# Two-layer vision kernel: the routing of the next batch is emitted between z and the FFN of the current one

## The chip, the cores and the metric

The kernel runs on one core of a Trainium2 chip. Its engines are TensorE (PE, matmuls; PEld is its weight load), VectorE (DVE), ScalarE (ACT), GpSimd (POOL) and SyncE (SP, which issues most DMAs). The metric is the device time of one launch in microseconds. The kernel before takes 4330.48 us, the median of three runs (4320.04 to 4338.9).

## What is computed

Four images of 384 channels and 32x32 pixels go through two layers in float32. Each layer is a mixing step and a feed-forward step, both with a residual.

```python
# layer 0
x = x + gelu(layernorm(selective_scan_in_four_directions(ln_c(x))))
t = to_tokens(x)                                   # 4 x 1024 tokens of 384
probs = softmax(ln_t(t) @ gate_w + gate_b)         # 4 experts, the best 2 of them kept
masked = probs * top2 ; masked /= masked.sum() + 1e-9
t = t + sum_e masked[e] * (gelu(ln_t(t) @ w1[e] + b1[e]) @ w2[e] + b2[e])
# layer 1
w = ln_c(x) @ w_qkv.T                              # one matrix serves as q, k and v; 8 heads of 64
x = x + softmax(w w.T / 8) w @ w_out.T + b_out
h = gelu(ln_t(t) @ kron(c_fc_1, c_fc_2).T)         # 384 -> 1536, a Kronecker product of rank 1 on one side
t = t + h @ kron(c_proj_1, c_proj_2).T
```

The scan is a recurrence over 1024 positions with 16 states for each of 384 channels, in four directions.

## The kernel before

The work has two parts for each batch (image).

The **scan** (`scan_layer`) walks 4 batches x 4 directions x 2 halves of the positions. A unit of these has three blocks of 128 channels (`chunk`), and a chunk four groups of states. For each group POOL multiplies step size and B (`bx`, L440, and L468 for C on half of them), ACT takes the exponential `da` (L449), DVE runs the recurrence (L454) and multiplies by C (L461), and PE adds up the states into `acc` (L475). One such group is called a scan step below; a batch has 96. The inputs of a chunk come through DRAM in SP's queue (`dtr` L424, `bcs` L350, `dd` L405 and L406), with seven `dtr` buffers. `acc` lives in PSUM, `bx` has six buffers.

The **tail** of a batch is everything after its scan:
- `route`: zero the table of rows (`clear`, L610), load x1 (L649), transpose it on PE together with the gate's scores (`tt_ps`, L656), evict (ACT L642, DVE L643), take token statistics on DVE (L662), store the tokens (L664). Then rank the experts of each token (`places`: a chain of some 70 small DVE operations, with two matmuls `cnt_ps` at L753), load the tokens again (L677), normalise them on ACT (L678) and scatter each token to its two rows by indirect DMAs from POOL (L683, 16 of them).
- `experts`: eleven slots of 256 or 128 rows, each of one expert, known only at run time (L866 loads its number into SP). Weights (L875, L883), a gather (L899), its transposes (`xc_ps`, L910), two matmul blocks (L927, L942) with a gelu between.
- `combine` and `prologue`: gather the two results of a token and weigh them, then normalise and transpose.
- `attention`: scores L1051, exponential on ACT L1057, weighted sum L1097, and at the end of each pair of heads the division (L1073).
- `last_layers`: for each half, output projection plus residual (`o_ps`, L1149 and L1151), a normalisation across channels that ends in `z` (L1158 to L1180), and after both halves the FFN: `h_ps` (L1193), gelu (L1202), `f_acc` (L1210), `fo_ps` (L1218), output (L1221).

Engines take their instructions in order, so the order in the program decides. It isn't written out by hand: a scheduler places each instruction on its engine's queue by data dependences, by a priority (the order of emission, with `high_priority(offset=FORWARD)` moving a block ahead by 20000) and by a timeline that it keeps for itself. `between(b)` calls `tail_batch(b - 1)` after the scan of batch b, and the scheduler then lays the tail over the scan of the next batch. The tail of batch 3 comes last, with nothing beside it but what the tail of batch 2 has left.

The order of emission in a tail is: experts, combine, prologue, attention, then `between()`, which for batches 0 and 1 emits the routing of the next batch, and then `last_layers`. So the routing of batch 1 is emitted ahead of the last layers of batch 0, both with the same offset of priority.

Buffers: tag `k4` has five tiles of 3 KB per partition (`NARROW`). `x` and `xt` of the routing, `xs`, `xc` and `y` of the experts, `ex` of the attention, `xt`, `z`, `fy` and `out` of the last layers all take theirs from it. PSUM tiles of the tail come from tag p (three banks) and tag o (one bank), `NARROW_BANKS`. The ranking's scratch area `places` takes the bank of tag o for its whole length, and so do `y_ps`, `o_acc` and `f_acc`. Tag `kw` (eight tiles of 4.5 KB) holds expert weights, and in turn attention's `w`, `vt` and `att` and the last layers' `wa`, `wb` and `wc`.

Of the kernel before, what the change touches and what calls it, by code (L numbers as in the profile page):

```python
# [18 lines left out]
B = 4  # L19
# [66 lines left out]
FORWARD = 20000  # L86
# [25 lines left out]
def halves(i):  # L112
    return slice(i * HF, (i + 1) * HF)


class Body:
# [380 lines left out]
    def tail_batch(self, b, x1, room):  # L497

        if b == 0:
            self.moe_consts(room)  # L500
            self.route(b, x1, room)
        xc = self.first_layer(b, room)
        self.second_layer(b, xc, room, lambda: b + 2 < B and self.route(b + 1, x1, room))

    def first_layer(self, b, room):

# [4 lines left out]

    def second_layer(self, b, xc, room, between):
        att = self.attention(xc, self.sums[:, b], room)
        between()
        with self.tc.high_priority(offset=FORWARD):
            self.last_layers(b, att, room)

    def overflow(self, room):

# [102 lines left out]
        )  # L622

    def route(self, b, x1, room):
        self.clear(b)
        with self.tc.high_priority(offset=FORWARD):
            self.place, self.slots = self.spread(b, x1, room)

    def spread(self, b, x1, room):


        nc = self.nc
        src = x1[b].rearrange("(c p) l -> p c l", p=P)
        st = room.tile([P, MB, 6], "r_st", "st")
        mv = room.tile([P, MB, 2], "r_mv", "mv")
        rstd = room.tile([P, MB], "r_rstd", "rstd")
        sc = room.tile([P, MB, NE], "sc", "sc")


        def evict(ps, xt, sc):  # L640
            ps = ps[:, :, : DC * (P + NE)].rearrange("p o (c e) -> p o c e", c=DC)
            nc.scalar.copy(xt.rearrange("p o (c e) -> p o c e", c=DC), ps[:, :, :, :P])  # L642
            nc.vector.tensor_reduce(  # L643
                sc, ps[:, :, :, P:].rearrange("p o c e -> p o e c"), AX.X, ALU.add
            )

        for m in [*range(MB // 2, MB, 2), *range(0, MB // 2, 2)]:
            x = room.tile([P, DC, 2 * P], "k4", "x")
            nc.sync.dma_start(out=x, in_=src[:, :, m * P : (m + 2) * P])  # L649
            xt = room.tile([P, 2, D], "k4", "xt")  # L650

            for o in range(2):
                ps = room.bank("p", "tt_ps")
                cols = slice(o * P, (o + 1) * P)
                for c in range(DC):
                    nc.tensor.matmul(  # L656
                        ps[:, c * (P + NE) : (c + 1) * (P + NE)], x[:, c, cols], self.turn[:, c, :],
                        start=True, stop=True,
                    )
                evict(ps.unsqueeze(1), xt[:, o : o + 1, :], sc[:, m + o : m + o + 1, :])  # L660
            for o in range(2):
                nc.vector.bn_stats(st[:, m + o, :], xt[:, o, :])  # L662
                nc.vector.bn_aggr(mv[:, m + o, :], st[:, m + o, :])
            nc.sync.dma_start(out=self.tokens(b)[:, m : m + 2, :], in_=xt)  # L664
        self.inverse_root(rstd, mv[:, :, 1], self.eps5)
        nc.vector.tensor_mul(sc, sc, rstd.unsqueeze(2).to_broadcast([P, MB, NE]))
        nc.vector.tensor_add(sc, sc, self.bg.unsqueeze(1).to_broadcast([P, MB, NE]))
        less = self.less_mean(mv[:, :, 0], rstd, room, "r_less")
        pos, gate, expert = self.places(sc, room)

        placed = []
        for m in range(MB):
            if m % 2 == 0:
                xt = room.tile([P, 2, D], "k4", "xt")
                nc.sync.dma_start(out=xt, in_=self.tokens(b)[:, m : m + 2, :])  # L677
            nc.scalar.activation(  # L678
                xt[:, m % 2, :], xt[:, m % 2, :], AF.Identity,
                bias=less[:, m : m + 1], scale=rstd[:, m : m + 1],  # L680
            )
            for k in range(TOP):
                put = nc.gpsimd.indirect_dma_start(  # L683
                    out=self.rows[b][:, :],
                    out_offset=bass.IndirectOffsetOnAxis(ap=pos[:, k, m : m + 1], axis=0),
                    in_=xt[:, m % 2, :], in_offset=None,
                ).ins
                for other in placed:
                    self.tc.declare_no_dep(put, other, reason="rows of different tokens")
                for other in self.zeroed:  # L690
                    self.depend(put, other)
                placed.append(put)
        return (pos, gate), (expert, placed)

    def places(self, sc, room):

# [410 lines left out]
                    divide(t, atts[t])  # L1107
        return atts

    def last_layers(self, b, att, room):  # L1110

# [67 lines left out]
            zs.append(z)  # L1181


        ng = 6

        def hidden(i, at):
            hs = room.tile([P, ng, HF], "k12", "hs")
            early = None
            for f in range(at, at + ng, 2):
                banks = [room.bank("p", "h_ps") for _ in range(2)]  # L1190
                for o, ps in enumerate(banks):
                    rows = slice((f + o) % nq * KR, ((f + o) % nq + 1) * KR)
                    ins = nc.tensor.matmul(  # L1193
                        ps, fc1[rows, (f + o) // nq, :], zs[i][rows, :], start=True, stop=True
                    ).ins
                    if o == 0 and early is not None:
                        self.depend(ins, early)
                done = [
                    nc.scalar.copy(hs[:, f - at + o, :], ps).ins for o, ps in enumerate(banks)  # L1199
                ]  # L1200
                early = done[0]
            self.exp_again(nc.scalar.activation(hs, hs, AF.Gelu).ins)  # L1202
            return hs

        for i in range(NH):
            out = room.bank("o", "f_acc")
            for at in range(0, FC, ng):
                hs = hidden(i, at)
                for f in range(at, at + ng):
                    nc.tensor.matmul(  # L1210
                        out[f % nq * KR : (f % nq + 1) * KR, :], pj1[:, f, :], hs[:, f - at, :],
                        start=(f < nq), stop=(f >= FC - nq),
                    )
            y = room.tile([P, HF], "k4", "fy")
            nc.vector.tensor_copy(y, out)
            for c in range(DC):
                ps = room.bank("p", "fo_ps")
                nc.tensor.matmul(ps, pj2[:, c * P : (c + 1) * P], y, start=True, stop=True)  # L1218
                o = room.tile([P, HF], "k4", "out")
                nc.vector.tensor_add(o, ps, x2[:, c, halves(i)])  # L1220
                nc.sync.dma_start(out=a["out"][b][c * P : (c + 1) * P, halves(i)], in_=o)  # L1221
# [128 lines left out]
def build(nc, a):  # L1350
    with tile.TileContext(nc, schedule_with_timeline_sim=True) as tc, ExitStack() as ctx:
        body = Body(ctx, tc, a)
        dram = ctx.enter_context(tc.tile_pool(name="x1", bufs=1, space=DRAM))
        x1 = [dram.tile([D, L], F32, tag=f"x1_{b}", name=f"x1_{b}") for b in range(B)]
        with ExitStack() as tail:
            room = body.open_tail(tail)

            def between(b):
                if b > 0:
                    body.tail_batch(b - 1, x1, room)  # L1360

            with ExitStack() as banks:
                room.open_banks(banks, NARROW_BANKS)
                body.scan_layer(x1, between)
                wide = Room(tc, tail, "w", WIDE)
                wide.open_banks(banks, NARROW_BANKS)
                body.route(B - 1, x1, wide)
                xc = body.first_layer(B - 1, wide)
            with ExitStack() as banks:
                wide.open_banks(banks, WIDE_BANKS)  # L1370
                body.second_layer(B - 1, xc, wide, lambda: None)
                flag = body.overflow(wide)
        over = nc.values_load(flag[0:1, 0:1], min_val=0, max_val=1)
        with tc.If(over > 0):
            body.second_layer_exact()
# [82 lines left out]
```

## Time and profile before

| what | us |
|---|---|
| median of 3 runs | 4330.48 |
| the profiled execution | 4328.09 |
| its span, first to last instruction | 4326.3 |
| busy: PE / DVE / ACT / POOL | 3343.5 / 2860.4 / 2517.2 / 3021.3 |
| POOL multiply `bx`, L440, 768 of 2364 ns | 1794.6 |
| POOL multiply `bx`, L468, 384 of 2364 ns | 906.0 |
| ACT exponential `da`, L449, 1536 of 690 ns | 1045.1 |
| expert matmuls L927 and L942 | 664.8 + 643.2 |
| attention matmuls L1051 and L1097 | 306.2 + 285.9 |

Where the stages of the tails begin and end on PE, by the times of their matmuls in the trace (us from the span's start):

| batch | `tt_ps` of its routing | experts (L927, L942) | attention (L1051, L1097) | `o_ps` | FFN (`h_ps` to `fo_ps`) |
|---|---|---|---|---|---|
| 0 | 679 to 799 | 876 to 1310 | 1366 to 1635 | 1725 to 1774 | 1786 to 1885 |
| 1 | 1637 to 1703 | 1898 to 2335 | 2397 to 2680 | 2726 to 2794 | 2810 to 2906 |
| 2 | 2681 to 2701 | 2917 to 3344 | 3401 to 3723 | 3724 to 3771 | 3788 to 3916 |
| 3 | 3482 to 3498 | 3558 to 4008 | 4052 to 4212 | 4213 to 4247 | 4256 to 4319 |

The scan runs from 44 to 3448 us: batch 0 alone until 747, the other three with a tail beside each of them. A busy time is a sum over stages with different limits, so a share of the whole span says little: what a change in one stage is worth is read from that stage. In a row of groups the columns are line, engine and operation, result and operands, count, busy time, mean of one, and the idle time before it with what ended it. In a row of waits they are who waited, for whom, the us in total, how many times, and the longest.

### The profile page before, as it was taken

The page shows a single profiled execution, that of the slowest core. Times are in us where ns is not written, and L with a number is a line of the kernel's source. Part 1 is how long each engine was busy: PE and PEld are TensorE (multiplying, and loading weights), DVE is VectorE, ACT ScalarE, POOL GpSimd, SP SyncE. Part 2 cuts the span into 40 slices and gives each one's busy share as a digit, 9 for nine tenths or more (in the row PEclk, how much of TensorE's full clock was granted, in tenths as well). Part 3 has the DMA queues.
Part 4 walks back from the last instruction along what each step waited for, and adds up shares of the span by engine and source line. Part 5 has one row for each costly group of instructions (what it writes and reads, how often), then busy time and mean ns, then how long its engine had stood idle before and what let it go on. Part 6 is the DMA issues. An engine that isn't in the chain of part 4 may idle for free. (4 is left out here: it accounts for less than half of the span.)

```text
span 4326.3 us, 45583 instructions
## 1 busy us (share of the span) xinstructions
PE 3343.5 (77%) x13244; PEld 1557.7 (36%) x13244; DVE 2860.4 (66%) x4200; ACT 2517.2 (58%) x4484; POOL 3021.3 (70%) x1471
## 2 busy tenths in 40 slices
PE   6445454388997895779996887669998889999896
PEld 2111111155552222235553222216555235566322
DVE  5999997878786868678886778777887720000101
ACT  5555555456665776566764777476666654344354
POOL 5999997798898968889898689778899810000100
PEclk8666666599998997879998999769998999999997
DMA  5444564567895535558789335547889343345100
GB/s 141 129 120 129 138 166 113 178 198 228 232 278 142 138 113 167 156 157 241 220 235 269 112 100 149 160 121 210 242 227 297 99 157 105 109 141 203 50 26 19
DMA packets 410322, 693.69 MB, mean 160 GB/s; under 512 B 51024, under 2 KB 209616, under 8 KB 410064
## 3 DMA queue, kind: packets, MB, share of 16 engines
q1 hardware_dynamic: 400752, 664.29, 52.9%
q0 software_dynamic: 8192, 25.17, 1.8%
q8 instruction: 106, 1.74, 0.2%
q14 instruction: 152, 1.25, 0.1%
q10 hardware_dynamic: 1120, 1.25, 0.1%
HBM read 569.00 MB, written 121.50 MB: 160 GB/s over the span
## 5 line engine op out<-in xcount | busy, mean ns | idle before, releaser
L440 POOL TENSOR_TENSOR bx<-dtr,bcs 128x1024 f32<-128x1024 f32 x768 | 1794.6, 2364 | 202.1 <-PE acc L475 109.4
L449 ACT ACTIVATE da<-dtr,nega 128x512 f32<-128x512 f32 x1536 | 1045.1, 690 | 940.0 <-DVE bx L461 574.9
L468 POOL TENSOR_TENSOR bx<-bx,bcs 128x1024 f32<-128x1024 f32 x384 | 906.0, 2364 | 154.1 <-DVE carry L465 70.6
L475 PE MATMUL acc<-bx,sel 128*32 128x512 f32 x3072 | 501.5, 709 | 319.1 <-POOL bx L468 270.7
L927 PE MATMUL h_ps<-xc,w 128*128 128x256 f32 (+1 forms) x3168 | 664.8, 365 | 64.5 <-DMA w<-in_w 20.2
L942 PE MATMUL y_ps<-w,hs 128*128 128x384 f32 x1824 | 643.2, 505 | 46.7 <-ACT hs L935 39.8
L927 PEld LDWEIGHTS h_ps<-xc,w 128*128 128x128 f32 x3168 | 549.9, 197 | 236.8 <-issue 95.0
L454 DVE TENSOR_TENSOR_SCAN bx<-da,carry,bx 128x512 f32<-128x512 f32 x384 | 473.4, 1270 | 117.3 <-POOL bx L440 62.5
L454 DVE TENSOR_TENSOR_SCAN bx<-da,bx 128x512 f32<-128x512 f32 x384 | 452.4, 1211 | 120.1 <-ACT da L449 66.3
L454 DVE TENSOR_TENSOR_SCAN da<-da,carry,bx 128x512 f32<-128x512 f32 x384 | 476.5, 1273 | 80.0 <-ACT da L449 67.9
L461 DVE TENSOR_TENSOR bx<-da,bcs 128x512 f32<-128x512 f32 x768 | 510.5, 680 | 3.7
L454 DVE TENSOR_TENSOR_SCAN da<-da,bx 128x512 f32<-128x512 f32 x384 | 455.0, 1219 | 55.8 <-ACT da L449 44.9
L942 PEld LDWEIGHTS y_ps<-w,hs 128*128 128x128 f32 x1824 | 349.9, 196 | 334.7 <-issue 74.3
L1057 ACT ACTIVATE ex<-s_ps 128x512 f32<-128x512 f32 x512 | 299.9, 590 | 159.7 <-PE s_ps L1051 157.9
L1051 PE MATMUL s_ps<-w 64*128 64x512 f32 x1024 | 306.2, 657 | 56.7 <-ACT ex L1057 55.1
L963 POOL TENSOR_TENSOR diag<-ident,g_weight 128x1024 f32<-128x1024 f32 x8 | 15.1, 1901 | 453.9 <-PE xc_ps L910 440.7
L932 ACT ACTIVATE hs<-h_ps,bb 128x256 f32<-128x256 f32 (+1 forms) x528 | 201.1, 440 | 181.9 <-PE h_ps L927 178.1
L1097 PE MATMUL o_acc<-ex,vt 128*64 128x512 f32 x1024 | 285.9, 633 | 20.0 <-ACT ex L1057 15.7
L475 PEld LDWEIGHTS acc<-bx,sel 128*32 128x32 f32 x3072 | 76.4, 117 | 617.6 <-POOL bx L468 378.3
L946 DVE TENSOR_TENSOR y<-y_ps,bb 128x384 f32<-128x384 f32 x76 | 41.6, 548 | 236.6 <-PE y_ps L942 236.5
L365 PE MATMUL dt_ps<-xd,wdt 108*128 108x512 f32 x192 | 125.5, 741 | 85.5 <-ACT mag L404 53.3
L1051 PEld LDWEIGHTS s_ps<-w 64*128 64x128 f32 x1024 | 82.3, 188 | 255.3 <-ACT ex L1057 211.8
(217 smaller groups left out, 3605.0 us busy)
## 6 DMA issues: line engine op xcount, KB each, us to landing
w<-in_w SPq DMA_DIRECT2D x352, 576.0 KB
dtr<-dd SPq DMA_DIRECT2D x1536, 128.0 KB
bcs<-both SPq DMA_DIRECT2D x512, 128.0 KB
dd<-one_e SPq DMA_DIRECT2D x96, 256.0 KB
dd<-mag SPq DMA_DIRECT2D x96, 256.0 KB
rows<-zero SPq DMA_DIRECT2D x76, 192.0 KB
xt<-x SPq DMA_DIRECT2D x32, 384.0 KB
xs<-rows SPq DMA_DIRECT2D x32, 384.0 KB
```

Of the source, the lines that this page charges most:

```text
L440: pool = nc.gpsimd.tensor_mul(bx, dtr[q][1], bc[:, 0].unsqueeze(1).to_broadcast([P, 2, HF])).ins
L449: nc.scalar.activation(da, dtr[q][0][:, j, :], AF.Exp, scale=nega[:, col : col + 1])
L454: nc.vector.tensor_tensor_scan(run(h), run(da), run(bx[:, j, :]), 0.0 if first else hold, ALU.mult, ALU.add,)
L461: dve = nc.vector.tensor_mul(bx[:, j, :], h, cg).ins
L468: pool = nc.gpsimd.tensor_mul(bx, bx, cg.unsqueeze(1).to_broadcast([P, 2, HF])).ins
L475: nc.tensor.matmul(acc[lo : lo + DB, :], sel, out[q][:, j, :], start=(g == 0), stop=(g == NG - 1),)
L927: nc.tensor.matmul(ps[:, r, :], w1[(f + r) // wf][:, c, (f + r) % wf * P : ((f + r) % wf + 1) * P], xc[:, c, :], start=(c == 0), stop=(c = ...
L932: nc.scalar.activation(hs[:, f + r, :], ps[:, r, :], AF.Identity, bias=bb[:, f + r : f + r + 1])
L942: nc.tensor.matmul(out[:, :D], hs[:, f, t * P : (t + 1) * P], w2[f // wf][:, f % wf, :], start=(f == 0), stop=(f == FC - 1),)
L1051: ins = nc.tensor.matmul(ps, w[rows, j * P : (j + 1) * P], w[rows, halves(i)], start=True, stop=True).ins
L1057: done.append(nc.scalar.activation(ex[:, o, :], ps, AF.Exp, scale=HD**-0.5, accum_out=sums[:, t, 2 * j + o, i : i + 1],).ins)
L1097: ins = nc.tensor.matmul(out[cols, :], made[t][1][:, j, cols], ex[:, o, :], start=(j == 0), stop=(j == MB - 1),).ins
```

## The change

For batches 0 and 1 the routing of the next batch is no longer emitted between attention and the last layers. It is handed into `last_layers` as two steps (`first`: zeroing, transposes and statistics up to the new `yield`; `second`: ranking and scatter), which run one after the other where both `z` tiles are emitted and the FFN is not. `spread` becomes a generator for that. For batches 1 and 2 the routing takes no priority offset of its own (it is inside that of `last_layers` already), and the zeroing DMAs now come under it too. For the first half of the FFN `f_acc` takes a bank of tag p instead of tag o in those two batches. The routing of batch 0 and of batch 3 is emitted where it was.

```diff
@@ -498,9 +498,10 @@
 
         if b == 0:
             self.moe_consts(room)
-            self.route(b, x1, room)
+            for step in self.route(b, x1, room):
+                step()
         xc = self.first_layer(b, room)
-        self.second_layer(b, xc, room, lambda: b + 2 < B and self.route(b + 1, x1, room))
+        self.second_layer(b, xc, room, self.route(b + 1, x1, room))
 
     def first_layer(self, b, room):
 
@@ -511,9 +512,8 @@
 
     def second_layer(self, b, xc, room, between):
         att = self.attention(xc, self.sums[:, b], room)
-        between()
         with self.tc.high_priority(offset=FORWARD):
-            self.last_layers(b, att, room)
+            self.last_layers(b, att, room, between if b < 2 else ())
 
     def overflow(self, room):
 
@@ -622,9 +622,22 @@
         )
 
     def route(self, b, x1, room):
-        self.clear(b)
-        with self.tc.high_priority(offset=FORWARD):
-            self.place, self.slots = self.spread(b, x1, room)
+
+        def forward():
+            return nullcontext() if 0 < b < B - 1 else self.tc.high_priority(offset=FORWARD)
+
+        parts = self.spread(b, x1, room)
+
+        def first():
+            self.clear(b)
+            with forward():
+                next(parts)
+
+        def second():
+            with forward():
+                self.place, self.slots = next(parts)
+
+        return first, second
 
     def spread(self, b, x1, room):
 
@@ -662,6 +675,7 @@
                 nc.vector.bn_stats(st[:, m + o, :], xt[:, o, :])
                 nc.vector.bn_aggr(mv[:, m + o, :], st[:, m + o, :])
             nc.sync.dma_start(out=self.tokens(b)[:, m : m + 2, :], in_=xt)
+        yield
         self.inverse_root(rstd, mv[:, :, 1], self.eps5)
         nc.vector.tensor_mul(sc, sc, rstd.unsqueeze(2).to_broadcast([P, MB, NE]))
         nc.vector.tensor_add(sc, sc, self.bg.unsqueeze(1).to_broadcast([P, MB, NE]))
@@ -690,7 +704,7 @@
                 for other in self.zeroed:
                     self.depend(put, other)
                 placed.append(put)
-        return (pos, gate), (expert, placed)
+        yield (pos, gate), (expert, placed)
 
     def places(self, sc, room):
 
@@ -1107,7 +1121,7 @@
                     divide(t, atts[t])
         return atts
 
-    def last_layers(self, b, att, room):
+    def last_layers(self, b, att, room, between=()):
 
 
 
@@ -1181,6 +1195,8 @@
             zs.append(z)
 
 
+        for step in between:
+            step()
         ng = 6
 
         def hidden(i, at):
@@ -1203,7 +1219,7 @@
             return hs
 
         for i in range(NH):
-            out = room.bank("o", "f_acc")
+            out = room.bank("p" if between and i == 0 else "o", "f_acc")
             for at in range(0, FC, ng):
                 hs = hidden(i, at)
                 for f in range(at, at + ng):
@@ -1364,11 +1380,12 @@
                 body.scan_layer(x1, between)
                 wide = Room(tc, tail, "w", WIDE)
                 wide.open_banks(banks, NARROW_BANKS)
-                body.route(B - 1, x1, wide)
+                for step in body.route(B - 1, x1, wide):
+                    step()
                 xc = body.first_layer(B - 1, wide)
             with ExitStack() as banks:
                 wide.open_banks(banks, WIDE_BANKS)
-                body.second_layer(B - 1, xc, wide, lambda: None)
+                body.second_layer(B - 1, xc, wide, (None, None))
                 flag = body.overflow(wide)
         over = nc.values_load(flag[0:1, 0:1], min_val=0, max_val=1)
         with tc.If(over > 0):
```

The last layers of the fallback path and of batches 2 and 3 get no steps: `between if b < 2 else ()`. Line numbers in the text are those of the kernel before.

## The prediction

> **What bounds the kernel now.** I read the page first, then a table of busy time by stage, then the waits of the two stretches that the change touches. The page, its span and two rows of the slices:
>
> ```profile
> span 4326.3 us, 45583 instructions
> ...
> PE   6445454388997895779996887669998889999896
> ...
> POOL 5999997798898968889898689778899810000100
> ```
>
> The reader is to see two regimes. Up to slice 31 GpSimd (POOL) is near full: that is the scan of the four batches. After it POOL is empty and TensorE (PE) is full: what the tail has left. The table by stage (columns: stretch, its length, busy us of each engine, granted clock, DMA share, GB/s):
>
> ```profile
> 44.00:750.00 706.00, 352.18 (x1076) 94.01 (x1080) 633.61 (x852) 376.41 (x587) 674.34 (x296) 0.67 0.49 131
> 750.00:1637.00 887.00, 708.49 (x2956) 345.01 (x2949) 696.54 (x1008) 569.21 (x1050) 755.04 (x370) 0.89 0.65 188
> 1637.00:1897.00 260.00, 161.10 (x561) 58.19 (x559) 199.88 (x336) 157.39 (x235) 217.21 (x111) 0.74 0.53 154
> 1897.00:2681.00 784.00, 674.55 (x2856) 329.84 (x2857) 614.74 (x870) 529.21 (x985) 669.84 (x321) 0.94 0.66 189
> 2681.00:2917.00 236.00, 154.30 (x511) 55.34 (x507) 180.76 (x293) 132.75 (x201) 183.55 (x94) 0.76 0.50 148
> 2917.00:3448.00 531.00, 470.13 (x2023) 271.75 (x2027) 431.99 (x582) 347.38 (x579) 476.51 (x228) 0.95 0.76 220
> ...
> 3558.00:4008.00 450.00, 438.90 (x1801) 269.02 (x1799) 34.55 (x62) 181.79 (x319) 3.79 (x2) 0.99 0.40 135
> ```
>
> Rows three and five are what I call the two transitions: from the end of attention of batch 0 (1) to the first expert matmul of batch 1 (2). There PE is idle for 98.9 and 81.7 us, and POOL for 260 - 217.2 = 42.8 and 236 - 183.6 = 52.4 us, 95.2 of 496 us or 19.2%. In the other three stretches that hold scan and tail together POOL is idle for 132.0 + 114.2 + 54.5 = 300.7 of 2202 us, 13.7%. So the tail is late by latency there, and it costs the scan more than elsewhere. The last row is the PE-bound end: 438.9 of 450 us busy. Who waits in the first transition, POOL then PE:
>
> ```profile
> POOL bx L468 <- DVE bx L454: 13.0, 4, 6.1
> POOL bx L440 <- PE acc L475: 9.1, 4, 6.0
> ...
> PE tt_ps L656 <- DMA x<-x: 11.7, 1, 11.7
> PE xc_ps L910 <- DMA xs<-rows: 9.5, 1, 9.5
> PE h_ps L1193 <- ACT hs L1199: 9.2, 4, 5.6
> PE f_acc L1210 <- ACT hs L1202: 9.1, 3, 4.4
> ```
>
> Waits of routing (`tt_ps`), gather (`xc_ps`) and FFN (`h_ps`, `f_acc`) stand one after the other on PE. No single wait is large; the scan's `acc` matmuls stand behind them.
>
> **What the Trainium skill says.** "PSUM — Partial Sum Buffer", Engine vs sequencer instructions: ScalarE, VectorE and GpSimd take their queues strictly first in, first out, and matmuls start in program order. The trace agrees: in the second transition the scan's copy of `mag` on ACT waits 14.6 us for a `places` operation of the routing on DVE. "DMA: Bandwidth & Descriptors", Queues, rings and completion order: on each DMA engine the descriptors of one issuing queue are consumed in ring order, so a small load stands behind larger ones issued before. The trace fits it only loosely (the `xt` load behind nothing still cost `o_ps` 4.6 us). "Perfetto Trace Analysis", Optimization Strategy: where the most contended engine changes over time, interleaving the regimes may help; the first two regimes here are already interleaved, and what moves is how much of the PE regime lies under the POOL regime.
>
> **The change part by part.** The order of the built programs' instructions, which holds no time, I count in scan steps (four `acc` matmuls of L475; 96 per batch). On PE:
> - transition 0 before: attention ends at 187, `tt_ps` 187-196, `cnt_ps` 199, `o_ps` 199-202, `h_ps` 203-211, first expert matmul 213. After: `o_ps` 187-192, `tt_ps` 195-196, `cnt_ps` 199, `h_ps` 199-203, experts 208. So 26 steps become 21.
> - transition 1 before: 299, `tt_ps` 299-301, `cnt_ps` 304, `o_ps` 304-308, `h_ps` 310-317, experts 320. After: 295, `o_ps` 295-299, `tt_ps` 302-304, `cnt_ps` 307, `h_ps` 307-314, experts 316. 21 steps in both, begun four earlier.
>
> Routing isn't earlier in either; the first half of the last layers is, and the FFN now lies over ranking and scatter, where the `o_ps` to `z` part lay before.
>
> Removed and added: no matmul, DMA, DVE or POOL instruction. ACT gets two more table loads (one at L230, one at L152): 2 x 1.283 us = 2.6 us (row L148, 68 loads of 1283 ns). "ScalarE: Activation LUTs", What ACT_TABLE_LOAD costs, gives the same 1283 ns. ACT is 61% busy in the transition; I take 1 us, bounds 0 and 2.6.
>
> Moved, for each transition: 48 `tt_ps` records (8.9 us, row L656), 8 evictions (3.7), 8 statistics (4.4), 8 normalisations of 694 ns on ACT (5.1), some 70 ranking operations on DVE of mostly 0.2 us, 16 scatters of 976 ns plus 4.6 us between them (20 us of POOL), 12 loads and stores on SP, 19 zeroing DMAs of 192 KB. These last cost nothing: they go from SP step 175 to just before it and from 271 to 267, a hundred us before routing needs them. All of the rest is paid in both kernels; only its neighbours differ.
>
> (1) Less left after the scan. Behind the last `acc` matmul stand 4 `s_ps`, 6 `o_acc`, 6 `w_ps`, 4 `v_ps` and 16 `bc_ps` fewer than before. From the chain of waits (2 `s_ps` 1.06, 2 `o_acc` 1.01, 6 `w_ps` 5.35, 8 transposes 1.02, 16 `bc_ps` 1.75 us): 2.1 + 3.0 + 5.4 + 0.5 + 1.8 = 12.8 us. PE is 97.5% busy there: -13 us, and under the scan this piece is free as long as POOL is the bound. Bounds -13 and 0.
>
> (2) The scan's own time in the transitions. If they stalled POOL like the other stretches, 496 x (19.2 - 13.7)% = 27 us would go. The reason for it: FFN waits and ranking waits now share the same time instead of following each other. The reason against: the tail's instructions per scan step rise in transition 0. I take half, -14 us; bounds -48 (half of all 95 us) and +47.
>
> (3) The k4 pool has five buffers of 3 KB per partition; the two `z` tiles hold two while routing runs, where before all five were routing's. So the fourth `xt` load goes into the first `z` buffer and waits for the last `h_ps` of the first FFN half. SP holds that load behind seven expert weight loads (7 x 576 KB = 4.0 MB), and all later loads behind it; ACT has its two normalisations after the second gelu of the FFN, with the scan's `da` behind; POOL issues the last four scatters apart from the first twelve. At 154 GB/s (row three) to 226 GB/s (during the scatters before) 4.0 MB take 18 to 26 us. They are issued as soon as the experts are known, on DVE at step 202, and the normalisations stand at 203.5: some 15 us, of them 5.3 for the gelu with its two table loads. So ACT may wait 3 to 11 us, and POOL, which runs ahead of ACT by its six `bx` buffers, less. I take 0, upper bound 20 us of POOL for each transition.
>
> (4) `f_acc` of the first half takes one of three p banks, leaving two for the `h_ps` pair. `h_ps` waits for ACT 9.2 us now; at worst it doubles, half of which reaches POOL: 0 taken, bound 5 us each.
>
> Sum: 4328.1 (the profiled execution; its span 4326.3) - 13 - 14 + 1 = 4302. The median of the runs is 2.4 above: 4304 us.
>
> **The rivals.**
> A, the forecast: 4304, own range 4285 to 4318; chance 0.40.
> B, no measurable change: the transitions stall as before, because routing isn't earlier and only the order within the transition changed, so only (1) is got, 4330 - 13 = 4317. This is also the case in which the change doesn't do what it says: `cnt_ps` stays at step 199, and goes from 304 to 307. Chance 0.27.
> C, slower: (3) decides. The wait of the last `xt` pair takes the place of the waits removed: ACT holds it, `da` stops behind it, then the DVE scan and POOL. With 20 us in each transition, and 3.5 each for (4): 4330 - 13 + 40 + 7 = 4364. It decides from about 17 us per transition. For it: three free buffers for routing's twelve tiles, weights ahead on SP, PE already waiting 9.5 us for the gather that follows. Against: the cover of 15 us, and the buffers ahead of POOL. Chance 0.20.
> D, a larger gain: half of all transition stalls go, since experts also start with rows and weights already there (the first gather stands at SP step 215, not 219): 4330 - 13 - 48 = 4269. Chance 0.13.
>
> **How the numbers follow.** Half a per cent, 21.7 us, is about what a measurement of this kernel can tell from no change. A and D count as faster, 0.53; B as same, 0.27; C as slower, 0.20. The range takes most of D below and half of C above: 4256 to 4360.
>
> **What would show it.** The stretch from the end of attention 0 to the first expert matmul should shrink from 260 us to about 225, with POOL idle there under 40; transition 1 stays near 230. The scan ends between 3430 and 3440 instead of 3448, and from there to the end it is 865 instead of 878. C shows as ACT waiting for the DMA of `xt` (L678 before) and POOL waiting at the scatter. I am wrong if the scan ends later than 3455, or if the stretch after it doesn't shrink.

## The result, and the profile after

The change takes 4301.23 us (median of six runs, 4296.73 to 4310.35) against 4332.39 us before on the same chip: ratio 0.9935, 95% interval 0.9915 to 0.9955. The profiled execution fell from 4328.09 to 4300.74 us, 27 us. In the change every line number from `spread` on is 13 to 16 higher. The page of the kernel after, its span and one row of the slices:

```profile
span 4299.0 us, 45575 instructions
...
POOL 5999997898898968789898978888989810000100
```

The two regimes are as they were; the border between them stands in the same slice. The table by stage, kernel after (stretch, its length, busy us of PE, PEld, DVE, ACT, POOL, granted clock, DMA share, GB/s):

```profile
1632.00:1851.00 219.00, 153.04 (x530) 58.63 (x526) 165.07 (x297) 134.40 (x201) 172.92 (x91) 0.74 0.54 164
...
2645.00:2866.00 221.00, 146.67 (x507) 52.61 (x505) 176.29 (x304) 134.94 (x204) 190.44 (x97) 0.74 0.53 161
2866.00:3429.00 563.00, 493.90 (x2129) 280.55 (x2129) 458.12 (x627) 369.39 (x625) 507.50 (x243) 0.93 0.73 212
...
3540.00:3981.00 441.00, 427.21 (x1761) 267.09 (x1759) 34.62 (x62) 175.10 (x298) 3.79 (x2) 0.99 0.41 138
```

Length says little here. Transition 0 went from 260 to 219 us, yet POOL is idle in it for 219 - 172.9 = 46.1 us, where it was 42.8: less scan lies in a shorter stretch. Transition 1 went only from 236 to 221, and its idle time from 52.4 to 30.6 us. POOL's work itself is the same in both kernels (2307 and 2308 us from 750 us to the scan's end), so the scan's end moves by POOL's idle time and by nothing else. That gives the sum that I use for all runs, within 4 us: the scan ends at 3057 us plus POOL's idle time since 750 us (before 3453 = 3057 + 396), and what stands behind it is the rest. I take the scan's end at the end of the last multiply of L468, which is 3453 before and 3434 after.

The longest wait of POOL in transition 1 of the kernel before lies in one stretch. All waits from 2786 to 2816 us, largest first (who waits, for whom, us, times, longest):

```profile
ACT x L1155 <- PE o_ps L1151: 19.3, 1, 19.3
DVE x_sq L1165 <- PE x_mean L1160: 18.6, 1, 18.6
POOL bx L440 <- PE acc L475: 12.8, 1, 12.8
...
PE o_ps L1149 <- DVE z L1180: 5.4, 1, 5.4
...
PE o_ps L1151 <- DMA xt<-x: 3.1, 1, 3.1
```

This is one standstill of all engines. ACT and DVE, in order, stand at the eviction and at `x_sq` of the last layers' second half, with the scan's `da` and recurrences behind them; `acc` is late and POOL stops. PE waits for little in it: 5.4 us for the first half's `z`, ahead of `o_ps`, and 3.1 us for the residual (`xt`, L1142, a `k4` tile). The rest of the time it works on this half: `o_ps` ends at 2800 us (the 2794 in the table of stages counts L1149 alone), then come `x_mean` and `z_ps`. So of the 18.6 us that DVE stands at `x_sq`, the residual is 3.1; the rest is the length of the chain, which DVE and ACT have in their queues ahead of the scan's work. The timeline of SP's queue shows when the two residual loads of that half (L1143) go out, and the row of the expert numbers says when SP read these (eleven reads, shortest, median and longest in ns, first and last start in us):

```profile
2784.62 0.00 SPq L1143 DMA_DIRECT2D xt<-x  x1
...
2792.04 0.48 SPq L1143 DMA_DIRECT2D xt<-x  x1
...
L866 SPq TENSOR_LOAD <-g_expert x11: 5/277/916, 2763.4 to 2779.7; - x11
```

The first load stands behind the expert numbers of the next batch, the second behind weight loads that wait for `o_ps` themselves (L875, 4.7 us in all). Routing, emitted ahead, holds `k4` tiles until its scatters are done, the last of which runs on POOL until 2783 us. That may be why the scheduler placed the loads so late; when SP reaches them, the trace shows no wait for a tile. In the change these loads are emitted ahead of routing, and both go out together:

```profile
2672.16 0.90 SPq L1157 DMA_DIRECT2D xt<-x  x2
```

The same `x_sq` wait in the two transitions was 15.7 and 18.6 us before, and is 2.8 us and absent after. Some waits of POOL in transition 1, kernel before:

```profile
POOL bx L440 <- PE acc L475: 14.0, 2, 12.8
POOL bx L468 <- DVE carry L465: 11.3, 5, 5.4
POOL bx L440 <- DMA dtr<-dd: 6.4, 2, 4.4
```

and kernel after:

```profile
POOL bx L468 <- DVE carry L465: 8.6, 3, 5.3
...
POOL bx L440 <- PE acc L475: 2.6, 2, 2.2
```

`acc` fell from 14.0 us to 2.6, and the waits for `dtr` are gone. In transition 0 the `acc` wait rose, from 9.1 to 16.3 us, and the gain there is nil, though the `x_sq` wait fell by 12.9 us there too.

### The profile page after: what moved, and what is told of

The parts are those of the page before. It is cut to its first block, busy times and chain, and to the rows that moved or that the text cites. A ratio compares the mean times of both kernels' runs of the same rounds, so it can differ in the third digit from the quotient of the medians.

```text
span 4299.0 us, 45575 instructions
## 1 busy us (share of the span) xinstructions
PE 3329.5 (77%) x13244; PEld 1560.8 (36%) x13244; DVE 2852.0 (66%) x4200; ACT 2516.4 (59%) x4486; POOL 3020.0 (70%) x1471
## 5 line engine op out<-in xcount | busy, mean ns | idle before, releaser
L468 POOL TENSOR_TENSOR bx<-bx,bcs 128x1024 f32<-128x1024 f32 x384 | 903.7, 2357 | 154.6 <-DVE carry L465 67.3
```

The costliest lines, as they stand in the source:

```text
L468: pool = nc.gpsimd.tensor_mul(bx, bx, cg.unsqueeze(1).to_broadcast([P, 2, HF])).ins
```

## The experiments

Theory O: the change gains in each transition because FFN and ranking waits share the same time. Theory L: it gains because less PE work is left behind the scan. The twelve kernels ran on three chips, where the kernel before takes 4310 us (experiments 1 and 2), 4309 (3 and 4) and 4333 (5), so I compare ratios to the kernel before on the same chip.

**1. The move in one transition at a time.**

```diff
-            self.last_layers(b, att, room, between if b < 2 else ())
+            inside = b == 0                 # second kernel: b == 1
+            if b < 2 and not inside:
+                for step in between:
+                    step()
+            self.last_layers(b, att, room, between if inside else ())
...
```

Further down, the routing that isn't moved gets its own priority offset back. The bank of `f_acc` goes with the move.

> Only the routing of batch 1 is emitted between z and the FFN (of batch 0); the routing of batch 2 stays ahead of the last layers of batch 1. Theory O (overlap: the gain is made in each transition, by laying ranking and scatter under the FFN and the first half of the last layers ahead of the transposes): about half of the gain of 31 us, 4310 to 4320 against 4332 before; transition 0 about 220 us, transition 1 as before, about 236. Theory L (leftover: what counts is only how much PE work the planner leaves behind the last scan step, wherever the change is made): 12 scores, 10 weighted sums, 6 projections and 16 divisions fewer than before are left, 6.4 + 5.0 + 5.4 + 1.0 + 1.8 = 20 us, so 4312, and more than the full change (13 us) gets after the scan.

> Only the routing of batch 2 is emitted between z and the FFN (of batch 1). Theory O: the other half of the gain, 4310 to 4320; transition 1 about 222 us, transition 0 as before, 260. Theory L: the planner leaves 16 scores and 16 weighted sums more than before behind the scan, 8.5 + 8.1 = 17 us: 4349, slower than before although the overlap is there.

Measured: only the first 0.9981 [0.9971, 0.9991], only the second 1.0087 [1.0068, 1.0105]. The parts don't add up to the whole, and the move in transition 1, where the profile had shown the gain, makes the kernel slower by itself. Theory O in its simple form falls; theory L has both signs, but not the sizes (0.995 and 1.004 forecast). In the second kernel transition 1 does get better (idle 40.6 us), but batch 3's scan behind it gets worse (84.7 us against 54.7), and the rest grows.

**2. The bank alone, and the zeroing alone.** Both against the kernel before:

```diff
-            out = room.bank("o", "f_acc")
+            out = room.bank("p" if ahead and i == 0 else "o", "f_acc")   # ahead = b < 2
```

> The kernel before with the bank of f_acc alone changed: tag p for the first FFN half of batches 0 and 1, routing where it was. Theory O: no gain, since nothing is overlapped anew; two banks instead of three for h_ps cost 0 to 10 us: 4332 to 4342. Theory L: 12 scores, 12 weighted sums, 6 projections, 8 transposes and 16 divisions fewer are left behind the scan, 21 us: 4311, more after the scan than the change itself.

```diff
-        self.clear(b)
+        with self.tc.high_priority(offset=FORWARD if 0 < b < B - 1 else 0):
+            self.clear(b)
```

> The kernel before with the zeroing DMAs of batches 1 and 2 alone moved under the priority offset. Theory O: 4332 within 0.3%, the zeroing is needed by nobody for a hundred us. Theory L: 6 scores and 6 weighted sums more are left behind the scan, 6 us: 4338. A change of more than 15 us either way would say that the planner's order alone moves the time as much as the change does.

Measured: bank alone 0.9955 [0.9939, 0.9971]; zeroing alone 1.0002 [0.9988, 1.0016]. The bank, which I had put at nothing, brings about as much without the move as the whole change brings. Its gain lies in the rest (849 us; 867 in the kernel before again, on a chip of about the same speed), not in the scan.

**3. Both kernels once more, and the move without the bank.**

> The kernel before once more, for a trace from the chip of the other runs: both theories expect 4310 within 15 us; its scan end and what follows say how far one trace of the same program differs from another (3453 and 874 in the first one).

> The whole change once more, beside the other runs. Theory O and theory L alike: ratio 0.9935 as before. If theory L has the size right, what follows the scan's end is 13 us less than in the run of the kernel before, and the rest of the gain is scan time.

```diff
-            out = room.bank("p" if between and i == 0 else "o", "f_acc")
+            out = room.bank("o", "f_acc")
```

> The change with f_acc left in tag o: routing between z and the FFN, but the first f_acc must wait until the ranking's scratch area lets the bank go. Theory O: the overlap of ranking and FFN is broken, so most of the gain goes: ratio 0.998 to 1.002. Theory L: 12 scores, 10 weighted sums, 6 projections, 8 transposes and 16 divisions fewer than before are left behind the scan, 20 us: ratio 0.9955, what follows the scan about 853 us.

Measured: the kernel before again 4312.37 us (one run; its median there is 4308.87), the change again 0.9947 [0.9926, 0.9968], the move without the bank 1.0047 [1.0031, 1.0063]. So the square is: neither 1, bank 0.9955, move 1.0047, both 0.9947. The move without its bank makes the kernel slower, and with the bank it adds nothing that the intervals can tell from the bank alone. Both theories missed the move without the bank (0.998 to 1.002 and 0.9955).

The two new traces are a second pair of before and after. Transition 1 gains as much as in the first (45.1 to 25.7 us of POOL's idle time), and the `x_sq` wait of 18.9 us goes in the same way. But `acc` is a small part of it. Waits of POOL in transition 1, the kernel before again:

```profile
POOL bx L468 <- DVE carry L465: 12.1, 6, 5.4
...
POOL bx L440 <- PE acc L475: 5.2, 1, 5.2
POOL bx L440 <- DMA dtr<-dd: 4.9, 2, 4.2
```

and the change again:

```profile
POOL bx L468 <- DVE carry L465: 6.7, 3, 4.7
...
POOL bx L440 <- PE acc L475: 2.4, 2, 2.2
```

Of the 19.4 us `acc` gives 2.8, `carry` 5.4 and `dtr` 4.9: the gain is spread over several waits. Scan and rest of the change and of the move without the bank, two rows each; first the change again:

```profile
752.00:3418.00 2666.00, 2162.20 (x8978) 1061.16 (x8974) 2120.43 (x3092) 1743.26 (x3074) 2305.40 (x1123) 0.90 0.65 190
3418.00:4285.00 867.00, 788.31 (x3145) 394.41 (x3145) 90.25 (x230) 379.21 (x797) 38.41 (x37) 0.94 0.30 102
```

and the move without the bank:

```profile
752.00:3474.00 2722.00, 2182.24 (x9015) 1074.08 (x9011) 2134.33 (x3093) 1746.55 (x3084) 2304.68 (x1124) 0.89 0.64 186
3474.00:4330.00 856.00, 778.76 (x3115) 389.15 (x3107) 89.55 (x229) 374.46 (x786) 38.43 (x38) 0.94 0.30 102
```

POOL's busy time is the same to 0.7 us; the scan ends 56 us later and the rest is 11 us shorter. The 56 us are POOL's idle time: more in both transitions (51.3 against 44.4 and 43.1 against 25.7), and most of all in batch 3's scan (72.5 against 44.5). In transition 1 of that kernel the largest wait of DVE is:

```profile
DVE fy L1231 <- DMA rows<-xt,g_pos: 13.1, 1, 13.1
```

`fy` is the next tile of `k4` after routing's, so the FFN's eviction waits there for a scatter to land, with the scan's recurrences queued behind it on DVE. In the change the `fy` waits of transition 1 are 6.4 us in one trace and 6.1 in the other. That this wait is what costs is not shown: in the next experiment `fy` waits 17.1 us in the same transition (for `acc`, by the trace), and POOL is idle for only 31.8.

**4. The `z` tiles out of `k4`.**

```diff
-            z = room.tile([P, HF], "k4", "z")
+            z = room.tile([P, HF], "kw" if between else "k4", "z")
```

> The change with the two z tiles in tag kw for batches 0 and 1, so that routing has all five k4 tiles and the fourth load of tokens need not wait for the FFN. Theory O: ACT's two waits of 9.5 us for that load go, 5 to 10 us of the scan: ratio 0.9915 to 0.9925. Theory L: 30 scores, 28 weighted sums, 6 projections, 8 transposes and 16 divisions fewer than before are left behind the scan, 15.9 + 14.1 + 5.4 + 1.0 + 1.8 = 38 us: ratio 0.991, what follows the scan about 835 us.

Measured: 0.9937 [0.9913, 0.9962], no different from the change on that chip. This tests step (3) of the prediction. The wait of ACT for the fourth `xt` load in transition 0, kernel after:

```profile
ACT xt L692 <- DMA xt<-x: 9.5, 1, 9.5
```

With `z` elsewhere it is gone, and a wait for `h_ps` has grown in its place, from 4.5 us in the kernel after (6.1 in the change again):

```profile
ACT hs L1215 <- PE h_ps L1209: 15.6, 6, 7.0
```

The wait for the fourth `xt` load was there, 9.5 us, and goes with the tiles; POOL's idle time in that transition stays (46.1 and 44.4 with the wait, 45.3 without), so taking it away gained nothing there. As another wait of ACT took its place, that doesn't show that it cost nothing. What this kernel gains is again in the rest, 826 us, and it is given back in the scan (388 us idle against 361 and 376).

**5. Routing under nothing, routing split, `z` alone, and a combination.** The expectations here count POOL's idle time with a constant of 3098 us in place of 3057, so their 350 for the kernel before is about the 396 of the table below. Routing behind the whole of the last layers, with `f_acc` in o:

```diff
-        for step in between:
-            step()
         ng = 6
...
+        for step in between:
+            step()
```

> The routing of the next batch emitted behind the whole last layers (batches 0 and 1), f_acc in tag o. So the last layers are early, as in the change, but ranking and scatter lie under nothing. Theory O: both transitions end later on PE (27 and 28 steps instead of 26 and 21), ratio 1.003 to 1.008. Theory L with the sum 3098 us + POOL's idle time + what follows the scan: 16 scores and 16 weighted sums more are left than before, 17 us, what follows is 887; with POOL idle for 350 as in the kernel before 4335, ratio 1.005; the idle time may be 20 us off either way.

The first step behind attention, the second between z and FFN:

```diff
+        if b < 2:
+            with self.tc.high_priority(offset=FORWARD):
+                between[0]()
         with self.tc.high_priority(offset=FORWARD):
-            self.last_layers(b, att, room, between if b < 2 else ())
+            self.last_layers(b, att, room, between[1:] if b < 2 else ())
```

> Only the second step (ranking and scatter) between z and the FFN; the first (transposes, statistics) behind attention, where all of it was before. Theory O: ranking is under o_ps, z and FFN, as good as the change or better: ratio 0.990 to 0.995, by POOL idle 320 to 330 like the change. Theory L: 8 scores, 6 weighted sums, 6 projections, 8 transposes and 16 divisions fewer than before are left, 15 us, what follows is 855; with POOL idle for 350 as before 4303, ratio 0.9965.

The `z` tiles of batches 0 and 1 in `kw` in the kernel before, and the same with the move of batch 1's routing alone (experiment 1):

```diff
-            z = room.tile([P, HF], "k4", "z")
+            z = room.tile([P, HF], "kw" if b < 2 else "k4", "z")
```

> The kernel before with the two z tiles of batches 0 and 1 in tag kw and nothing else. Theory O: routing is over when z is made, so nothing is gained: ratio 1.000 to 1.002. Theory L: 2 scores and 2 weighted sums fewer left, 2 us: ratio 0.9995; POOL idle decides the rest. A ratio of 0.9935, as with z moved in the change, would say that it is the placement of z that pays.

> The routing of batch 1 alone moved, with both z tiles in tag kw; chosen because the order leaves least behind the scan: 44 scores, 44 weighted sums, 12 projections, 16 transposes and 32 divisions fewer than before, 23 + 22 + 11 + 2 + 3.5 = 62 us. Theory L: what follows the scan 810; with POOL idle for 345 the sum is 4253, ratio 0.987, better than the change. Theory O: half of the change's gain, ratio 0.997, and at best that of the change, 0.9947.

Measured: behind the FFN 1.0158 [1.0136, 1.0180], split 1.0003 [0.9991, 1.0015], `z` alone 1.0033 [1.0015, 1.0051], the combination 0.9934 [0.9912, 0.9957]. The last was chosen because its built order leaves least PE work behind the scan, and it does have the shortest rest (824 us). Against the mean of the two traces of before it wins 46 us in the rest and gives 19 back in the scan. It stays short of theory L's 0.987, and the first two miss both theories; `z` alone says that the placement of `z` doesn't pay by itself. Against theory L's sums the scan came 21 to 38 us late in these three kernels, and the rest was 9 to 14 us longer. No version beats the change by more than the intervals allow.

All traces side by side, in us: POOL's idle time in five stretches (750 to the end of attention 0, transition 0, from there to the end of attention 1, transition 1, from there to the scan's end; each is length less POOL busy), its sum, the rest, and the PE work left behind the scan against the kernel before. The last is counted in the built order and priced as in step (1) of the prediction.

| kernel | 750 on | tr. 0 | middle | tr. 1 | last | sum | rest | left |
|---|---|---|---|---|---|---|---|---|
| before | 132.0 | 42.8 | 114.2 | 52.4 | 54.7 | 396.1 | 873.5 | 0 |
| before again | 132.5 | 40.0 | 114.8 | 45.1 | 57.2 | 389.6 | 867.3 | 0 |
| the change | 126.3 | 46.1 | 117.5 | 30.6 | 55.6 | 376.1 | 864.8 | -12.8 |
| the change again | 130.5 | 44.4 | 115.5 | 25.7 | 44.5 | 360.6 | 867.2 | -12.8 |
| first only | 136.5 | 44.6 | 105.4 | 49.3 | 58.2 | 394.0 | 852.4 | -19.5 |
| second only | 126.5 | 40.0 | 108.3 | 40.6 | 84.7 | 400.1 | 884.3 | +16.6 |
| bank alone | 133.3 | 39.8 | 106.2 | 48.4 | 73.0 | 400.7 | 849.2 | -20.5 |
| zeroing alone | 127.6 | 40.1 | 119.1 | 37.7 | 62.9 | 387.4 | 872.0 | +6.2 |
| move without bank | 125.5 | 51.3 | 125.0 | 43.1 | 72.5 | 417.4 | 855.6 | -19.5 |
| `z` elsewhere | 127.6 | 45.3 | 120.9 | 31.8 | 62.8 | 388.4 | 826.1 | -38.2 |
| behind the FFN | 132.4 | 48.6 | 128.6 | 49.8 | 72.3 | 431.7 | 901.1 | +16.6 |
| split | 125.8 | 39.5 | 122.0 | 43.8 | 81.4 | 412.5 | 864.1 | -15.4 |
| `z` alone | 133.4 | 40.7 | 115.1 | 47.0 | 62.3 | 398.5 | 882.5 | -2.1 |
| first only, `z` in `kw` | 130.2 | 50.4 | 125.3 | 47.5 | 58.5 | 411.9 | 824.4 | -61.8 |

Two things follow. The rest obeys theory L: a straight line through the 14 points has a slope of 0.94 us per us of work left, with a correlation of 0.94. Chips differ too: on those where the kernel before takes 4332 or 4333 us (before, the change, and the four kernels of experiment 5) the rest lies some 11 us higher for the same work left. Within each of the two groups of chips the correlation is 0.96 and 0.98, and the slope 0.96 and 0.94; a difference of 10 us between rows of different groups says nothing. The scan's idle time doesn't follow the work left at all (correlation 0.03). The bank of `f_acc` alone, which touches neither routing's place nor its data, moves it by 57 us between the change again and the move without the bank. Where ranking and scatter lie under no part of the last layers (behind the FFN) both sums are worst, and 28 of its 60 us against the trace of before are the rest.

## Why the prediction was right, and where not

The forecast was 4304 us, and the sum of -26 us against -27 in the profiled execution. The direction, the size and rival A hold. The terms don't hold as well as their sum: one was too large, one too small and at the wrong place, and the one put at nothing decided the sign. That the sum came out within 1 us is luck.

**(1), less left behind the scan: -13 forecast.** Measured -8.7 in the pair of traces of the result (873.5 to 864.8) and -0.1 in the other, -4 in the mean. A stretch after the scan that doesn't shrink was named as a sign of being wrong, and in the second pair it doesn't (867.3 and 867.2). The mechanism holds over all kernels, at 0.94 of its price; in the change it brought a third. The stretch of batch 3's experts did shrink, from 450 to 441 us, but part of that was lost on the way from the scan's end to it. As sized, the term was too large by 9 us.

**(2), POOL's idle time in the transitions: -14 forecast.** The scan's idle time fell by 20 us in the one pair and 29 in the other, -24.5 in the mean. The place was wrong. I looked for the gain in transition 0, because it would become shorter, with POOL idle there under 40 us. It became shorter as forecast (219 us for about 225), and the idle time rose by 3 us. The gain lies in transition 1, -20.6 us in the mean. The step that failed is to take one share of idle time for both transitions and to tie the gain to FFN and ranking waits lying side by side. What the trace of before shows there is the standstill from 2786 us, in which POOL waits 12.8 us for `acc` behind the second half of `o_ps`. That this standstill ends is not the whole of it. The `x_sq` wait goes in the second pair too, where `acc` gives only 2.8 of 19.4 us. It falls in transition 0, which gains nothing. And it is gone from transition 1 of three kernels that gain less there: second only (40.6 us idle), split (43.8) and behind the FFN (49.8). So the runs show where the idle time fell, spread over `acc`, `carry` and `dtr`; its cause stays open.

**(3), the shortage of `k4`: 0 taken, ACT to wait 3 to 11 us.** ACT waited 9.5 and 9.4 us. With that wait gone from transition 0 and another in its place, POOL's idle time is the same, so no cost of it shows. The loads took 4.0 and 5.2 us from going out to ACT's start; for the rest of its wait the load hadn't gone out. The 4.6 us that the prediction gives for one `xt` load are two waits, 2.1 and 2.5 us. Rival C had the right wait and the wrong price: it needed 17 us in each transition.

**(4), the bank for `f_acc`: 0 taken, bound 5 us each.** This is the part that I misjudged most. I saw only the bank taken from the `h_ps` pair. The other side is the single bank of tag o, which `places` holds through the ranking: without the edit the first `f_acc` is ordered against it. With the move, the bank is worth 0.9947 against 1.0047, some 43 us; my bound of 10 us was far too narrow. Without the bank the change would have gone to the slower side, and rival C's wait doesn't tell the two kernels apart: in transition 0 ACT waits 11.4 us for the load without the bank and 9.9 with it, in transition 1 2.0 and 7.7. The bank alone, with routing where it was, gives 0.9955, in the rest where the change gains in the scan. So the edit that the prediction put at nothing brings by itself as much as the whole, and the move that it priced makes the kernel slower without it.

**The signs named.** The scan ends 19 us earlier by either way of reading its end. By the prediction's way, the start of the last pair of multiplies, it went from 3448 to 3429 (3430 to 3440 forecast), and the rest from 878 to 870 (865 forecast). That routing isn't earlier holds: `cnt_ps` starts at 1741 us instead of 1725, and at 2757 instead of 2726.

**What stays open.** Why the scan's idle time in batch 3's part lies at 44 to 57 us in the change and in the kernel before, and at 58 to 85 in all others, is not settled, nor why transition 1 gains and transition 0 doesn't: the scheduler lays a new order with each edit, and no run here holds that order fixed. So the square of experiment 3 shows what each edit brings in this program, not a cost of the bank or of the move as such.

## What to carry to other kernels

Split the time into parts that different things decide, here the bound engine's idle time and the work left behind it, and ask of each edit which part it moves: the two answered to different causes, and several edits won in one what they lost in the other. Where a scheduler sets the order, run the kernel before again, and each bundled edit alone, ahead of believing the mechanism; here a line that picks a PSUM bank decided the sign of the whole change. And follow one long wait of the bound engine to the first wait in its chain, but take it for the cause only if it goes where the time goes: here the same wait fell in both transitions, and one of them gained.

## What the hardware showed unexpectedly

Ranking operations of DVE with a few elements sometimes took as long as a POOL multiply. The timeline of DVE, kernel before again, in transition 1 (start us, us, instruction):

```profile
2739.24 2.08 DVE L832 TENSOR_TENSOR g_later<-slot_at_i,g_first 128x27 f32<-128x27 f32 x1
2741.24 2.38 DVE L832 TENSOR_TENSOR g_lone<-slot_at_i,g_first 128x9 f32<-128x9 f32 x1
...
2743.86 2.06 DVE L796 TENSOR_SCALAR g_full<-g_more 128x4 f32<-128x4 f32 x1
...
2746.49 1.71 DVE L844 TENSOR_TENSOR g_half<-g_ef,g_half 128x2 f32<-128x2 f32 x1
2748.12 2.37 DVE L847 TENSOR_TENSOR g_half<-g_half 128x1 f32<-128x1 f32 x1
```

The timeline of POOL there, six multiplies without a gap, 2.31 us each:

```profile
2736.61 13.87 POOL L440 TENSOR_TENSOR bx<-dtr,bcs 128x1024 f32<-128x1024 f32 x6
```

By 2.31 us these end at 2738.92, 2741.23, 2743.54, 2745.86, 2748.17 and 2750.48; the slow operations of DVE end at 2741.32, 2743.62, 2745.92, 2748.20 and 2750.49. Each finishes when the multiply beside it does. In the change again the same operations, DVE:

```profile
2769.71 1.75 DVE L846 TENSOR_TENSOR g_later<-slot_at_i,g_first 128x27 f32<-128x27 f32 x1
2771.38 0.16 DVE L846 TENSOR_TENSOR g_lone<-slot_at_i,g_first 128x9 f32<-128x9 f32 x1
...
2772.97 0.15 DVE L810 TENSOR_SCALAR g_full<-g_more 128x4 f32<-128x4 f32 x1
```

and POOL, one multiply that ends at 2771.41 us and then nothing for 5 us:

```profile
2769.07 2.34 POOL L440 TENSOR_TENSOR bx<-dtr,bcs 128x1024 f32<-128x1024 f32 x1 [0.17 <-PE acc L475]
2776.78 2.35 POOL L468 TENSOR_TENSOR bx<-bx,bcs 128x1024 f32<-128x1024 f32 x1 [5.37 <-DVE g_ends L823]
```

With POOL idle they take 0.15 us. In the transitions of both kernels I found 20 such operations (transition 1 in two traces each, transition 0 in one each), and all end within 0.08 us of the end of a multiply. The Trainium skill, "GPSIMD Engine Reference", Specifications, says that GpSimd's SBUF interfaces are shared with VectorE, with contention for DVE instructions in a 2-port mode or with two SBUF inputs. It fits this stretch: `g_later`, `g_lone` and both `g_half` take two inputs from SBUF. `g_full` has one, and the trace doesn't show in which mode it ran. Operations beside the same multiplies that took one of their inputs from PSUM were not held (`g_need`, L766, 0.19 us: its `places` is a PSUM tile). No run here moves an operand from one memory to the other, so this is seen and not tested. In this transition the busy time of the ranking (L716 to L855) fell from 21.0 us in both traces of before to 12.9 and 12.7. A chain of small operations cost more here where the bound engine was busy beside it.
